# Cross attention and a feed-forward layer on one core: the query projection as two levels of Strassen's product, in four PSUM streams

## The chip, the core and the metric

The kernel runs on one NeuronCore of a Trainium2 chip. Its engines work side by side, each through its own queue of instructions in order: TensorE (PE; its weight loads are listed as PEld), VectorE (DVE), ScalarE (ACT), GpSimd (POOL) and SyncE (SP), which here only starts transfers between DRAM and the on-chip memory SBUF. TensorE writes its products to PSUM, eight banks of 128 x 512 float32; VectorE and ScalarE take them out of there. Engines wait for each other by semaphores.

The metric is the device time of one execution in microseconds (us), as a median of several. A profile is one more execution, recorded instruction by instruction; its span is a little shorter than its time.

## The reference

Everything is float32. x is 8 x 128 x 512 (8 sequences of 128 tokens, 1024 tokens T), the context the same, with 32 heads of 128.

```python
def reference(x, ctx, mask, position_bias, ln_weight, w_q, w_k, w_v, w_out, Wg, Wu, Wd, ag, au, ad):
    h = layernorm(x)
    n = rmsnorm(h) * ln_weight
    q = (n @ w_q.T).reshape(b, 128, 32, 128)          # w_q, w_k, w_v: 4096 x 512
    k = (ctx @ w_k.T).reshape(b, 128, 32, 128)
    v = (ctx @ w_v.T).reshape(b, 128, 32, 128)
    score = einsum('bqhd,bkhd->bhqk', q, k) + position_bias
    p = masked_softmax(score, mask)
    attn = einsum('bhqk,bkhd->bqhd', p, v).reshape(b, 128, 4096)
    x = x + h + attn @ w_out.T
    y = layernorm(x)
    return x + ((silu(y @ Wg.T * ag) * (y @ Wu.T * au)) @ Wd.T) * ad
```

## The kernel before

Weights and context arrive with the contracted dimension first, so that a product needs no transposition but that of the normed tokens. The 32 heads go in 8 groups of 4; a group's weights for the queries, keys or values are one tile of 128 x 4 x 512 (1 MB).

All projections use one level of Strassen's product in Winograd's form (`seven`, L210): weights and tokens are cut into 2 x 2 blocks, sums of blocks are made first (`sums_a` L191 for weights, `sums_b` L199 for tokens), and seven block products, not eight, are added up in the output. For a group's queries (`project_T`, L254), a block of weights holds 256 contracted rows and 256 outputs, a block of tokens 256 contracted rows and 512 tokens; a block product is two output tiles by two contracted chunks, each a matmul 128 x 128 by 128 x 512, so a group has 28 matmuls. TensorE runs a float32 matmul as two passes: the profile lists 448 for the queries. One bank of PSUM takes products 1, 6, 7 and 4 in turn, each added to what is there, and is read out after each; another takes product 2, a third 5 and 3. Products 2, 6, 7, 4 are copied out by ScalarE (L235, L245), products 1, 5 and 3 added by VectorE (L240, L251). Tiles come in pairs, so TensorE fills one bank while the other is read.

The stages, in order:

1. Keys and values of group 0. In between, layer norm and RMS norm of the tokens (`norm1`, L159), their transposition on TensorE (`norm1_T`, L178) into `hT` (128 x 7 x 1024: four chunks of normed tokens and three of sums).
2. Queries of all groups, L412 to L422. Weights come from a pool of three tiles (`wpool`), two groups ahead where a tile is free; GpSimd makes a group's four weight sums (`combine_rows`, L206); the finished heads go to DRAM, four transfers of 512 KB a group, since SBUF can't hold them. In the last round the keys' weights of group 1 are loaded (`load_kv`).
3. Attention, group by group (`probabilities` L290, `transpose_p` L331, `attend` L350), with the keys and values of the next group between. A score needs queries (from DRAM), keys and bias: GpSimd adds bias and mask (L296), VectorE adds the scores (L304), then softmax, a transposition of the probabilities through DRAM, and the product with the values.
4. Output projection, residual, second norm, feed-forward.

`acts` is a pool of 18 tiles of 128 x 1024 for whatever is large and short-lived: inputs, heads, keys, values. `work` holds temporaries of the norm and of attention. PSUM has three pools of two tiles (`ps_mm`, `ps_tp`, `ps` with two tags). Instructions are put into each engine's queue by a scheduler, which takes them in about the order of the program but may move them; a tile is given out again when all that read it have finished, and the engine that writes it next waits for that. SyncE's transfers are issued in the order of its queue: one that waits holds up all behind it.

The weight sums on GpSimd (`eng` is GpSimd):

```python
    def sums_a(eng, a11, a12, a21, a22, s1, s2, s4):
        eng.tensor_tensor(s1, a21, a22, ADD)
        eng.tensor_tensor(s2, s1, a11, SUB)
        eng.tensor_tensor(a21, a11, a21, SUB)
        eng.tensor_tensor(s4, a12, s2, SUB)
        return {1: a11, 2: a12, 3: s4, 4: a22, 5: s1, 6: s2, 7: a21}
```

Of the kernel before, what the change touches and what calls it, by code (L numbers as in the profile page):

```python
# [25 lines left out]
def xattn_ffn_kernel(  # L26
# [45 lines left out]
    acts = pool("acts", 18, reuse_waits="tile")  # L72
    work = pool("work", 2, side="right", reuse_waits="tile")
    small = pool("small", 4, side="right", reuse_waits="tile")

    proj, rows, attn = ExitStack(), ExitStack(), ExitStack()
    toks = pools(proj)("toks", reuse_waits="tile")
    spool = pools(proj)("spool", 2, reuse_waits="tile")
    wpool = pools(proj)("wpool", 3, reuse_waits="tile")
    hpool = pools(rows)("hpool", side="right", reuse_waits="tile")  # L80
    ps_mm, ps_tp, ps = (pools(attn)(f"ps{n}", 2, space=PSUM) for n in ("mm", "tp", "at"))

# [9 lines left out]
    def load_q(g):  # L92
        return load_w(f"wq{g}", wqT[:, bass.ts(g, GW)])

    ctx_sb = toks.tile([P, DC + 3, T], F32, tag="ctx", name="ctx_sb")
    wk0 = wpool.tile([P, DC, GW], F32, tag="w", name="wk0")
    wv0 = wpool.tile([P, DC, GW], F32, tag="w", name="wv0")

# [20 lines left out]
    for b in range(B):  # L121
        nc.sync.dma_start(x_in[b // 2][:, b % 2, :], x[b])
    q_w = {0: load_q(0)}

    lnw_sb = const.tile([P, DC], F32, name="lnw_sb")
    nc.gpsimd.dma_start(lnw_sb, lnw.rearrange("(c p) -> p c", p=P))
    mask_u8 = work.tile([P, B, S], U8, tag="tt", name="mask_u8")
    nc.gpsimd.dma_start(mask_u8, mask.rearrange("b q k -> q b k"))
# [25 lines left out]

    hT = hpool.tile([P, DC + 3, T], F32, tag="hT", name="hT")
    mv1 = const.tile([P, B, 2], F32, name="mv1")
    rs1 = const.tile([P, B], F32, name="rs1")

    def norm1(b):  # L159
        st = small.tile([P, nc.vector.BN_STATS_DIM], F32, tag="st", name=f"st_{b}")  # L160
        xb = x_in[b // 2][:, b % 2, :]
        moments(mv1, b, st, xb)
        rs = rs1[:, b : b + 1]
        rstd_of(rs, mv1[:, b, 1:2], 1.0)
        y = work.tile([P, D], F32, tag="s", name=f"y_{b}", bufs=3)
        nc.vector.tensor_scalar(
            y, xb, mv1[:, b, 0:1], rs, ALU.subtract, ALU.mult
        )
        sq = work.tile([P, D], F32, tag="aT", name=f"sq_{b}")
        ss = small.tile([P, 1], F32, tag="ss", name=f"ss_{b}")  # L170
        nc.scalar.activation(sq, y, AF.Square, accum_out=ss)
        rr = small.tile([P, 1], F32, tag="rr", name=f"rr_{b}")
        rstd_of(rr, ss, 1.0 / D)
        hn = work.tile([P, D], F32, tag="pT", name=f"hn_{b}", bufs=4)
        nc.scalar.activation(hn, y, AF.Copy, scale=rr)
        return b, hn

    def norm1_T(b, hn):  # L178
        tp = transposed(hn, ps_tp.tile([P, DC, P], F32, tag="pt", name="tp"))
        nc.vector.tensor_tensor(  # L180
            hT[:, :DC, bass.ts(b, S)], tp, lnw_sb.unsqueeze(2).to_broadcast([P, DC, P]), ALU.mult
        )

# [22 lines left out]

    def combine_rows(name, w):

        a11, a12 = w[:, :HC, :HW], w[:, HC:, :HW]
        a21, a22 = w[:, :HC, HW:], w[:, HC:, HW:]  # L210
        s = spool.tile([P, 3, HC, HW], F32, tag="S", name=f"S_{name}")
        s1, s2, s4 = s[:, 0], s[:, 1], s[:, 2]
        return sums_a(nc.gpsimd, a11, a12, a21, a22, s1, s2, s4)

# [38 lines left out]

    def project_T(name, w, src, heads):  # L254

# [12 lines left out]

        yield from seven(name, range(2), product, part, ps_mm)

    def project_V(name, w, src, pairs, *banks):
# [16 lines left out]

        yield from seven(name, range(2), product, part, *banks)


# [79 lines left out]
    def kv(g, out):  # L371
        wk, wv = kv_w.pop(g)
        kT, v = [], []
        out[g] = kT, v
        keys = project_T(f"k{g}", combine_rows(f"k{g}", wk), ctx_t, kT)
        if g:
            yield from keys
            yield from project_V(f"v{g}", combine_rows(f"v{g}", wv), ctx_t, v, ps_mm)
        else:

            yield from itertools.islice(keys, 4)
            values = project_V(f"v{g}", combine_rows(f"v{g}", wv), ctx_t, v, ps, "sc")
            yield from itertools.islice(values, 4)
            yield from keys
            yield from values
# [6 lines left out]
    for n, _ in enumerate(kv(0, kvs)):  # L392
        if n % 2 == 1 and 5 <= n < 5 + 2 * B:
            normed.append(norm1((n - 5) // 2))
        if n % 2 == 1 and 11 <= n < 11 + 2 * B:
            norm1_T(*normed.pop(0))
    for n in normed:
        norm1_T(*n)
    h_t = combine_tokens(hT)

# [6 lines left out]
    for t, src in ((ag_sb, ag), (au_sb, au)):  # L407
        nc.sync.dma_start(t[:, :nf], src[: nf * P].rearrange("(c p) -> p c", p=P))
        if INTER % P:
            nc.sync.dma_start(t[: INTER % P, nf : nf + 1], src[nf * P :].unsqueeze(1))  # L410
    nc.sync.dma_start(ad_sb, ad.partition_broadcast(P))
    for g in range(NG):  # L412
        if g + 1 < NG:
            q_w[g + 1] = load_q(g + 1)
        else:
            kv_w[1] = load_kv(1)
        heads = []
        for _ in project_T(f"q{g}", combine_rows(f"q{g}", q_w.pop(g)), h_t, heads):
            pass
        for j in range(GH):  # L420
            nc.sync.dma_start(queries[g][:, j, :], heads[j])

    rows.close()

# [337 lines left out]
```

## Time and profile before

| | |
|---|---|
| time, median of 3 runs | 1153.86 us (1151.64 to 1154.1) |
| profiled execution | 1155.07 us |
| its span | 1153.3 us |
| TensorE busy | 1116.4 us, 97% |
| VectorE, ScalarE, GpSimd busy | 501.0, 317.4, 307.3 us |
| chain that ended last | 90% TensorE; 17% of the span is `mm_q` L261 |
| query stage | 69.2 to 261.5 us, one group 24 us |

The page counts busy time by engine and follows back the chain of waits that ended last. Groups of instructions give a line of the program, engine, operation, output and inputs with shapes, how often, busy time and the mean of one, and the idle time in front of them with what ended it. TensorE's ends are modelled, so spacing is a better measure of a matmul than its listed length: matmuls are pipelined, and a listed 592 ns of a 512-column pass overlaps its neighbours.

### The profile page before, as it was taken

Reading aid. Unit: us, or ns where it says so; the run is one execution under the profiler, and the core shown is the slowest. Engines: PE = TensorE matmul, PEld = TensorE weight load, DVE = VectorE, ACT = ScalarE, POOL = GpSimd, SP = SyncE. Lnnn points to the kernel's source line nnn. Section 1 sums busy time; section 2 is a strip of 40 time slices with the busy share of each in tenths; the row PEclk is TensorE's granted clock in tenths of the full one; section 3 lists DMA queues with packets and bytes.
Section 4 is the critical chain, followed back from the end, with each engine's and each line's share of the span. In section 5 each row is a group of like instructions: output and inputs, shape, how many; then the busy total and the mean of one; then the engine's idle time right before and its main releaser. Section 6 shows DMA issues by size and latency. Waiting matters only on the chain.

```text
span 1153.3 us, 12296 instructions
## 1 busy us (share of the span) xinstructions
PE 1116.4 (97%) x4286; PEld 729.4 (63%) x4286; DVE 501.0 (43%) x937; ACT 317.4 (28%) x889; POOL 307.3 (27%) x255
## 2 busy tenths in 40 slices
PE   6899999999999999999999999689999999999998
PEld 3564444445867677686858688578888864444445
DVE  4541111116555556555555557724433253433311
ACT  2521112223444344434344433301000022222000
POOL 5331221116333333333223314530000034330000
PEclk9999999999999999999999999899999999999999
DMA  9114423257646465555554446864222322110000
GB/s 281 43 37 149 178 110 110 109 204 252 187 138 200 145 192 162 176 181 174 184 172 148 135 146 199 256 217 170 92 92 80 116 99 73 36 37 1 15 31 28
DMA packets 117534, 154.38 MB, mean 134 GB/s; under 512 B 12033, under 2 KB 71681, under 8 KB 117473
## 3 DMA queue, kind: packets, MB, share of 16 engines
q1 hardware_dynamic: 114784, 149.93, 40.4%
q10 hardware_dynamic: 2192, 2.10, 0.6%
q0 software_dynamic: 496, 1.58, 0.4%
q8 instruction: 34, 0.56, 0.2%
q14 instruction: 28, 0.22, 0.1%
HBM read 101.14 MB, written 52.43 MB: 133 GB/s over the span
## 4 chain that ended last, share of the span: by engine, by line
PE 90%; DVE 4%; DMA 4%; issue 1%; ACT 1%; SPq 0%; ACTq 0%; DVEq 0%
PE mm_q L261 17%; PE mm_v L279 16%; PE mm_k L261 15%; PE m L469 15%; PE mm_f L688 9%; PE dn L712 7%; PE sc L301 4%; PE av L357 4%; DMA turned<-tt 1%; DMA wk<-in_wkT_dram 1%; DVE sg L640 1%; DMA a<-att 1%; DVE act L643 1%; PE tp L152 1%; PE up L654 1%
## 5 line engine op out<-in xcount | busy, mean ns | idle before, releaser
L296 POOL TENSOR_TENSOR s<-pb,mneg 128x512 f32<-128x512 f32 x64 | 81.2, 1269 | 290.7 <-DVE tt L334 234.0
L261 PE MATMUL mm_k<-ctx_sb,wk 128*128 128x512 f32 x256 | 117.4, 603 | 7.5 <-DMA wk<-in_wkT_dram 4.4
L279 PE MATMUL mm_v<-wv,ctx_sb 128*128 128x256 f32 x512 | 115.9, 379 | 1.3 <-DMA wv<-in_wvT_dram 1.3
L261 PE MATMUL mm_q<-hT,wq 128*128 128x512 f32 x256 | 112.5, 592 | 0.0
L469 PE MATMUL m<-wo,a 128*128 128x256 f32 x400 | 100.6, 389 | 9.6 <-DMA a<-att 9.1
L311 ACT ACTIVATE s<-s,nmx 128x128 f32<-128x128 f32 x256 | 99.5, 390 | 37.4 <-DVE nmx L308 37.4
L279 PEld LDWEIGHTS mm_v<-wv,ctx_sb 128*128 128x128 f32 x512 | 95.1, 190 | 14.8 <-DMA wv<-in_wvT_dram 2.1
L362 ACT COPY aT<-av 128x512 f32<-128x512 f32 x64 | 37.5, 586 | 202.9 <-PE av L357 98.5
L261 PE MATMUL mm_k<-ctx_sb,S_k 128*128 128x512 f32 x192 | 87.8, 605 | 4.4 <-DVE k L240 4.0
L469 PEld LDWEIGHTS m<-wo,a 128*128 128x128 f32 x400 | 77.1, 196 | 21.2 <-DMA a<-att 9.5
L261 PEld LDWEIGHTS mm_q<-hT,wq 128*128 128x128 f32 x256 | 48.6, 190 | 60.8 <-issue 60.7
L279 PE MATMUL mm_v<-S_v,ctx_sb 128*128 128x256 f32 x384 | 86.4, 381 | 0.0
L261 PEld LDWEIGHTS mm_k<-ctx_sb,wk 128*128 128x128 f32 x256 | 46.9, 193 | 60.4 <-issue 45.2
L261 PE MATMUL mm_q<-hT,S_q 128*128 128x512 f32 x192 | 85.0, 592 | 0.0
L304 DVE TENSOR_TENSOR s<-sc,s 128x512 f32<-128x512 f32 x64 | 44.2, 690 | 86.0 <-PE sc L301 82.9
L301 PEld LDWEIGHTS sc<-k,q 128*128 128x128 f32 x512 | 67.4, 194 | 17.9 <-issue 13.4
L279 PEld LDWEIGHTS mm_v<-S_v,ctx_sb 128*128 128x128 f32 x384 | 71.7, 190 | 10.6 <-DVE v L251 1.5
L712 PE MATMUL dn<-wd,act 128*128 128x512 f32 (+3 forms) x198 | 75.8, 545 | 0.0
L251 DVE TENSOR_TENSOR q<-q,mm_q 128x512 f32<-128x512 f32 x32 | 22.0, 688 | 114.8 <-PE mm_q L261 114.8
L301 PE MATMUL sc<-k,q 128*128 128x128 f32 x512 | 68.1, 277 | 2.8 <-DMA q<-queries 2.8
L357 PE MATMUL av<-pT,v 128*128 128x128 f32 x512 | 67.9, 277 | 0.0
L261 PEld LDWEIGHTS mm_k<-ctx_sb,S_k 128*128 128x128 f32 x192 | 35.6, 193 | 48.6 <-issue 35.7
(156 smaller groups left out, 1494.3 us busy)
## 6 DMA issues: line engine op xcount, KB each, us to landing
queries<-q SPq DMA_DIRECT2D x32, 512.0 KB, 3.8
q<-queries SPq DMA_DIRECT2D x32, 512.0 KB, 4.5
turned<-tt SPq DMA_DIRECT2D x64, 256.0 KB, 2.2
pT<-turned SPq DMA_DIRECT2D x256, 64.0 KB, 2.5
att<-aT SPq DMA_DIRECT2D x64, 256.0 KB, 2.3
a<-att SPq DMA_DIRECT2D x32, 512.0 KB, 3.4
wq<-in_wqT_dram SPq DMA_DIRECT2D x8, 1024.0 KB, 5.6
wk<-in_wkT_dram SPq DMA_DIRECT2D x7, 1024.0 KB, 6.2
```

The costliest lines, as they stand in the source:

```text
L251: nc.vector.tensor_tensor(part(r, c, t), part(r, c, t), m[t], ADD)
L261: nc.tensor.matmul(out, w[i][:, c, bass.ts(t, P)], src[i][:, c, :], start=(first and c == 0), stop=(c == HC - 1), skip_group_check=True,)
L279: nc.tensor.matmul(out[:, bass.ts(k, HW)], src[i][:, c, bass.ts(2 * t + k, S)], w[i][:, c, :], start=(first and k == 0 and c == 0), stop=( ...
L296: nc.gpsimd.tensor_tensor(s, pb, mneg[:, b : b + 1, :].to_broadcast([P, GH, S]), ALU.add)
L301: nc.tensor.matmul(sc[:, j, :], qT[:, j, bass.ts(b % 2, S)], kT[j][:, cols], start=True, stop=True)
L304: nc.vector.tensor_tensor(s, sc, s, ALU.add)
L311: nc.scalar.activation(s[:, j, :], s[:, j, :], AF.Exp, bias=nmx[:, j : j + 1], accum_out=sm[:, j : j + 1],)
L357: nc.tensor.matmul(av[:, j, :], v[b // 2][:, b % 2, bass.ts(j, P)], pT[:, :, j, :], start=True, stop=True,)
L362: nc.scalar.copy(aT, av)
L469: nc.tensor.matmul(m[n], sa[n][:, c, :], wo_t[g][n][:, c, :], start=(g == order[0] and c == 0 and k % 2 == 0), stop=(g == order[-1] and c ...
L688: nc.tensor.matmul(out, ws[t][n][:, c, :], h2_t[n][:, c, :], start=(first and c == 0), stop=(c == HC - 1), skip_group_check=True,)
L712: nc.tensor.matmul(o, act[ic][:m, bass.ts(b, S)], wd[:m, ic, cols], start=(n == 0), stop=(n == NI - 1),)
```

## The change

The query projection gets a second level: each of the seven block products is again cut into 2 x 2 and done as seven products, so a group has 49 products, each one matmul of 128 x 128 by 128 x 256 (one contracted chunk, one output tile, a quarter of the tokens). Each level saves one product in eight, so 49 replace 56 half-width ones.

The work around it changes with it:

- `hT` becomes 128 x 7 x 7 x 256: 7 outer by 7 inner blocks of tokens. `combine_tokens2` makes the outer sums and the inner ones, eight more VectorE instructions and one more on GpSimd, besides four (three of them on VectorE) that are made while the norm still runs.
- `combine_rows2` makes twelve weight sums a group on GpSimd in place of four: the outer four, four inner ones of the raw blocks, four of the three outer sums. It is called one group ahead. Weights, and all sums of them, are in two pools `qw`, group g in pool g % 2.
- `project_T2` runs the inner products as the outer loop (k = 2, 1, 6, 7, 4, 5, 3) and, for each, the seven outer products in four streams: A holds products 2 and 1, B 6 and 7, C 4 and 5, D product 3, each with two banks of PSUM. After each k the four banks are read out, ScalarE and VectorE as before. What is kept is not heads but seven outer products in eight `acts` tiles (`kept`).
- The outer additions (12 on VectorE, 2 on GpSimd per group) and eight stores of 256 KB per group form a list, which the next group's call works off.
- The stage's pools lie where those of attention come later, so `wpool`, `spool`, `work` and attention's PSUM pools are opened after it. The keys and values weights of group 1 and the bias are thus loaded after the stage; the keys of group 0 go to DRAM and come back; the mask is loaded into an `acts` tile.

```diff
-    q_w = {0: load_q(0)}
-    mask_u8 = work.tile([P, B, S], U8, tag="tt", name="mask_u8")
+    mask_u8 = acts.tile([P, B, S], U8, tag="a", name="mask_u8")
     nc.gpsimd.dma_start(mask_u8, mask.rearrange("b q k -> q b k"))
...
-    hT = hpool.tile([P, DC + 3, T], F32, tag="hT", name="hT")
+    hT = hpool.tile([P, 7, 7, 256], F32, tag="hT", name="hT")
...
+    def inner_tokens(v):
+        nc.vector.tensor_tensor(v[:, :, 4], v[:, :, 1], v[:, :, 0], SUB)
+        nc.vector.tensor_tensor(v[:, :, 5], v[:, :, 3], v[:, :, 4], SUB)
+        nc.vector.tensor_tensor(v[:, :, 6], v[:, :, 2], v[:, :, 5], SUB)
+    def inner_last(eng, v):
+        eng.tensor_tensor(v[:, :, 1], v[:, :, 3], v[:, :, 1], SUB)
+    def combine_tokens2():
...
+        nc.vector.tensor_tensor(quad(4), quad(1), quad(0), SUB)
+        nc.vector.tensor_tensor(quad(5), quad(3), quad(4), SUB)
+        nc.gpsimd.tensor_tensor(quad(1), quad(3), quad(1), SUB)
+        nc.vector.tensor_tensor(quad(6), quad(2), quad(5), SUB)
+        inner_last(nc.gpsimd, hT[:, 0:3:2])
+        for v in (hT[:, 4:7], hT[:, 1:4:2]):
+            inner_tokens(v)
+            inner_last(nc.vector, v)
+    def combine_rows2(name, w, pool):
+        outer = combine_rows(name, w, pool)
...
+        four = inner(lambda k, r: raw[:, :, :, k, r], *(i4[:, n] for n in range(3)))
+        rest = inner(lambda k, r: three[:, :, k, bass.ts(r, P)], *(i3[:, n] for n in range(3)))
...
+    STREAMS = {"A": (2, 1), "B": (6, 7), "C": (4, 5), "D": (3,)}
+    INNER = ((2, 1, 1), (1, 1, 1), (6, 1, 2), (7, 2, 2), (4, 2, 1), (5, 2, 2), (3, 1, 2))
+    def project_T2(name, w, dst, before):
+        for n, (k, r, c) in enumerate(INNER):
+            for tag, pair in STREAMS.items():
...
+                m = banks[tag]
+                for h, i in enumerate(pair):
+                    nc.tensor.matmul(
+                        m[:, h], w(i, k), hT[:, BLOCK[i], BLOCK[k]],
+                        start=(k in (2, 1, 5) and h == 0), stop=True, skip_group_check=True,
+                    )
...
+                to = kept[tag, r][:, c - 1]
+                if k in (1, 5, 3):
+                    nc.vector.tensor_tensor(to, to, m, ADD)
+                else:
+                    nc.scalar.copy(to, m)
+            if k not in (1, 5, 3):
+                for _ in range(6):
+                    if before:
+                        before.pop(0)()
...
+        for r in (1, 2):
...
+            add(nc.vector, m[2], m[1])
+            store(m[2], 0, 0, r)
+            add(nc.vector, m[6], m[1])
+        for r in (1, 2):
...
+            add(nc.vector, m[7], m[6])
+            add(nc.vector, m[6], m[5])
+            add(nc.gpsimd, m[5], m[7])
+            store(m[5], 1, 1, r)
+            add(nc.vector, m[4], m[7])
+            store(m[4], 1, 0, r)
+            add(nc.vector, m[6], m[3])
+            store(m[6], 0, 1, r)
+        return todo
...
+    keys0 = dram.tile([P, GH, T], F32, name="keys0")
+    for j in range(GH):
+        nc.sync.dma_start(keys0[:, j], kvs[0][0][j])
...
+    left, rows = [], combine_rows2("q0", load_q(0), qw[0])
     for g in range(NG):
+        now = rows
         if g + 1 < NG:
-            q_w[g + 1] = load_q(g + 1)
-        else:
-            kv_w[1] = load_kv(1)
-        heads = []
-        for _ in project_T(f"q{g}", combine_rows(f"q{g}", q_w.pop(g)), h_t, heads):
-            pass
-        for j in range(GH):
-            nc.sync.dma_start(queries[g][:, j, :], heads[j])
-    rows.close()
+            rows = combine_rows2(f"q{g + 1}", load_q(g + 1), qw[(g + 1) % 2])
+        left = project_T2(f"q{g}", now, queries[g], left)
+    for do in left:
+        do()
+    first.close()
...
+    kv_w[1] = load_kv(1)
+    for j in range(GH):
+        kvs[0][0][j] = acts.tile([P, T], F32, tag="a", name=f"k0_{j}")
+        nc.sync.dma_start(kvs[0][0][j], keys0[:, j])
```

## The prediction, made before the changed kernel ran

> **What bounds the kernel now.** I read the chain of waits first, in order of time, because it says which engine ended each stretch.
>
> ```profile
> 65.76 3.46 PE mm_v L279 x16
> 69.22 192.27 PE mm_q L261 x448
> 261.48 0.89 PE sc L301 x8
> ```
>
> Columns: start, length, what. TensorE alone makes up the query stage, from 69.2 to 261.5 us: 192.27 / 448 = 429 ns for one pass over 512 columns. The values' passes over 256 columns, each with fresh weights, take 3.46 / 16 = 216 ns, so half-width passes stream at the same rate; the weight load (190 ns in the groups of instructions) fits under them. The table by stage shows the other engines nearly idle in one 24 us group (117 to 141): VectorE 4.12 us, ScalarE 4.69, GpSimd 4.98. Next, what the helpers cost:
>
> ```profile
> L195 POOL TENSOR_TENSOR wq<-wq 128x512 f32<-128x512 f32 x8 | 10.1, 1268 | 0.0
> L195 POOL TENSOR_TENSOR wg<-wg 128x256 f32<-128x256 f32 x5 | 3.6, 730 | 0.0
> L717 DVE TENSOR_TENSOR r<-r,x 128x512 f32<-128x512 f32 x7 | 4.8, 691 | 0.2
> L245 ACT COPY q<-mm_q 128x512 f32<-128x512 f32 x48 | 28.1, 586 | 81.7 <-PE mm_q L261 81.7
> ```
>
> Busy time, then the mean of one in ns. And from the transfers, size and median us from issue to landing:
>
> ```profile
> wq<-in_wqT_dram SPq DMA_DIRECT2D x8, 1024.0 KB, 5.6
> ...
> wv<-in_wvT_dram SPq DMA_DIRECT2D x7, 1024.0 KB, 7.0
> ```
>
>  A GpSimd sum of 512 columns costs 1.27 us (starts 1.22 apart back to back), of 256 0.73, so 384 is about 1.0 (0.95 apart). VectorE sums start 0.60 apart. In the timelines of VectorE and GpSimd at the stage's start, both read two SBUF operands:
>
> ```profile
> 68.49 2.99 DVE L202 TENSOR_TENSOR hT<-hT 128x1024 f32<-128x1024 f32 x1
> ```
>
> ```profile
> 68.06 2.35 POOL L203 TENSOR_TENSOR hT<-hT 128x1024 f32<-128x1024 f32 x1 [11.93 <-DVE hT L201]
> 70.37 2.25 POOL L193 TENSOR_TENSOR S_q<-wq 128x512 f32<-128x512 f32 x1
> ```
>
> The VectorE sum, 1.23 us alone, waits for the GpSimd one to end at 70.4; the next GpSimd sum, 1.27 alone, then takes 2.25. They take turns. Last, the table by stage around TensorE's longest wait, 3.96 us up to 26.08 for VectorE's first keys addition (the last three columns: granted clock, DMA share, GB/s):
>
> ```profile
> 25.00:30.00 5.00, 3.92 (x6) 1.74 (x7) 5.00 (x17) 1.96 (x7) 5.00 (x5) 0.66 0.70 157
> ```
>
> A clock of 0.66 over 5 us: a wait this long costs another 0.34 x 5 = 1.7 us of matmul time.
>
> **What the change takes away.** 8 x 49 products, two passes each, are 784 passes x 216 ns = 169.6 us against 192.3: **-22.7 us**, 21.2 us a group. Only TensorE gains.
>
> **The new weight chain.** Per group GpSimd now does 4 outer sums of 512, 4 inner of 512, 4 inner of 384, then two additions for the results of the previous group. In the order in which the built program's instructions stand, SyncE's queue holds: load of weights g+2, eight stores of group g, load of g+3. Two of the stores wait for the two GpSimd additions; GpSimd does these only after all twelve sums for g+2, which wait for the load of g+2. So load, twelve sums, two additions, stores and next load form a ring, one turn per group. A turn P is:
> - five stores issued after the additions, 0.4 each (issues of this size take 0.32 to 0.38 and stand some 0.06 apart): 2.1 with the semaphore;
> - the load: 5.6 alone; it stands behind 1.25 MB of stores. The first weight load, behind eight input loads, took 7.4, value loads up to 10.1. I take 6.8, as its backlog is partly drained when it is issued;
> - sums 8 x 1.22 + 4 x 0.95 + 0.15 = 13.7;
> - VectorE's twelve SBUF sums per group: about five fall into GpSimd's stretch, 0.6 each: 3.0. Bounds 0 and 5.0 (eight);
> - two additions 2.5 and hops 0.2.
>
> Sum **P = 28.3 us**, bounds 24.1 and 33.7, against 21.2 of matmuls. Even the lower bound is above, so the ring sets the pace from group 3 on and TensorE waits.
>
> What TensorE waits for: the pool of 18 activation buffers, 4 held by the values, 8 filled per group. Group g's B copies on ScalarE (second stream, first round) need the buffer of group g-2's C results, freed only by those late stores. Behind that copy stand ScalarE's C and D copies, VectorE's B addition and stream B's product 6 on TensorE. From the additions' end to the end of that group's matmuls: 3.2 (stores issued and landed; 256 KB stores land in 2.2 to 2.3) + 1.4 (copy 0.59, addition 0.69, hops) + 33 products x 0.43 = 14.3 + 1.7 for the clock after the idle = 20.6.
>
> The Trainium skill (SBUF — State Buffer, "Who interferes with whom") has a VectorE instruction with two SBUF inputs and a GpSimd one that reads SBUF exclude each other for the whole instruction. Charged for all twelve sums at the trace's 0.69, that would be 8.3 us a turn instead of 3.0, so P 33.6 and a time near 1223 instead of 1197.
>
> **The start.** The mask's load was GpSimd's second instruction, at 2.17 us, landed by 9.55. It now stands behind six sums for keys and values and the context sum, about 26.7 us; with 3.6 to 7.4 to land (the software-queue loads), VectorE's mask instruction, now ahead of the first keys addition, ends at 31 to 35. That addition ran at 25.26; TensorE and ScalarE's norm chain hang on it. The idle of 3.96 us grows by 5.6 to 9.3; I take **+7**. Afterwards TensorE had no slack up to 69.2.
>
> Then the token sums: VectorE did 3 sums of 1024 after the last transposed tile; it now does those plus four of 512 and four of 768 (0.6, 0.88 apart: 5.9 us) before the first round's additions, which round three needs. From the trace the third sum of 1024 ends near 73.2; the rest at 79.1 alone, 85 if each waits for a GpSimd sum. Two rounds of TensorE from 69.2 end at 75.3: stall 4.6 to 10.5, **+8**, nearer the upper as GpSimd starts its sums at 75.
>
> **Adding up the stage**, in the old time scale (the +7 comes on top): group 0 ends at 69.2 + 21.2 + 8 = 98.4. Load 5.6, twelve sums 13.7, contention 1.5, one addition 1.2: additions of group 0 end at 120.4. Group 1's: two stores 0.8, load 5.9, sums 16.7, additions 2.5: 146.4. Four turns of 28.3: 259.6. Last matmuls: +20.6 = 280.2 against 261.3: **+18.9**.
>
> **The end of the stage.** Value weights 1 and bias used to be loaded during the stage. Both now wait for the stage's buffers, and on SyncE's queue for the last stores, thus for VectorE's ten last sums: 0.7 + 6.0 + 1.2 for turns with GpSimd = 7.9 after the last matmul; value load issued at 8.4, landed (7.4) at 15.8. GpSimd takes two value sums before the first bias + mask: 2.6 + 1.25; VectorE's scores 0.7; the third score product can go at 20.5. Until then TensorE has 1.8 of scores and 3.4 of keys: idle 15.3, where it idled 0.45 before; and 1.7 for the clock. **+17**, bounds 8 (the bias, landing in 3.3, not held up by the value loads and sums, and no loss of clock) and 20 (value load 10.1).
>
> Costed at nothing: the keys' round trip through DRAM (eight transfers of 512 KB, 3.8 and 4.5 us), issued twenty and more us ahead; ScalarE's copies (8.5 us a group) and VectorE's 6.5 + 7.2 us, under 28 us; hT written in halves (8 x 0.15 us), under the values' matmuls. Had that cover gone, the last is 1.2 us.
>
> **Sum**: 7 + 18.9 + 17 = +42.9 on the profiled execution's 1155.07 (span 1153.3 and 1.8 around it): 1198. That execution stands 1.2 above the median of 1153.86; I say **1197**.
>
> **Rivals.**
> - *The matmuls keep the pace, the ends cost what I say*: -22.7 + 8 + 7 + 17 = +9.3, 1164. For it: transfers overlap well elsewhere (131 GB/s here, 363 and more at the start). Against: GpSimd's fourteen instructions and one load alone are 13.7 + 2.5 + 5.6 = 21.8 > 21.2.
> - *Faster*: the ring stays hidden, in one place: if the loads land early enough that P is at most 21.2, the whole 22.7 comes home, and the ends at their lower bounds (4.6 + 5.6 + 8 = 18.2) leave -4.5: 1150.6. It decides only from P = 21.2 down and with ends under 22.7 in sum.
> - *The turn-taking is heavier, or loads crawl behind the stores*: P = 33.7, each turn +5.4, about five turns: +27, 1224. For it: the 2.25 and 2.99 us rows; against: most VectorE sums come when GpSimd awaits its load.
>
> **Chances and range.** Mine (1175 to 1214) 0.62; heavier turns 0.14; matmul pace with dear ends (1156 to 1175) 0.16; faster 0.06; no change 0.02. A difference counts from 0.2% (2.3 us), about what this kernel's measurement can tell. All lower bounds together give 1161, all upper ones 1237; both ends at once are unlikely: **1163 to 1224**.
>
> **What would show it.** In the new profile: mm_q passes of 216 ns, with TensorE idle in each group from the third on, put down to VectorE or ScalarE behind a store; weight loads one per 28 us; GpSimd sums near 1.27 with some at 1.9; the mask sum on VectorE after 30 us; TensorE idle some 15 us in the 20 us after the last mm_q. Group starts 21 us apart would make the forecast wrong, and so would weight loads issued while the twelve sums run.

## The result, and the profile after

The changed kernel takes 1208.36 us (median of four runs, 1202.59 to 1208.73) where the kernel before, run beside it, takes 1153.98: a ratio of 1.046, with a 95% interval of 1.0429 to 1.0491. It is slower by 54.4 us in the medians. The profiled execution is the fastest of the four, 1202.59 us (span 1200.8), which is 47.5 us above the profiled one of before; the working below goes by that one.

From the page of the kernel after, the busy times and the chain that ended last:

```profile
PE 1116.1 (93%) x4622; PEld 803.4 (67%) x4622; DVE 626.5 (52%) x1100; ACT 343.8 (29%) x953; POOL 422.9 (35%) x336
...
PE 69%; DVE 6%; DMA 3%; issue 1%; POOL 1%; ACT 1%; SPq 1%; DVEq 0%; ACTq 0%; POOLq 0%
```

TensorE was 97% busy and is 93%. The 69% of the chain can't be set beside the 90% of before: here the chain is followed back to 217.3 us only, and its shares add up to 82%. TensorE is busy as long as before (1116.1 us, before 1116.4), though it has less to do. In the stage it is busy 183.2 us where it was 192.4, and 13.9 us of that are more than the products need; in the hand-over to attention it is busy 37.1 where it was 30.4. The mean granted clock is 0.94 and 0.80 there, where both were 1.00: after the wait of 8.02 us below it is 0.50 and 0.58 for two microseconds each. Where it waits, from its timeline (start, length, what, and in brackets the idle time in front and what ended it):

```profile
32.27 5.64 PE L263 MATMUL mm_k<-ctx_sb,S_k 128*128 128x512 f32 x8 [11.33 <-DVE rs L143]
94.09 2.08 PE L357 MATMUL mm_q_A<-hT,i_q 128*128 128x256 f32 x4 [8.02 <-DVE q_A L367]
185.62 1.27 PE L357 MATMUL mm_q_A<-hT,i_q 128*128 128x256 f32 x4 [3.79 <-DVE q_A L367]
188.92 2.08 PE L357 MATMUL mm_q_B<-hT,i_q 128*128 128x256 f32 x4 [2.03 <-DVE q_B L367]
312.88 1.65 PE L416 MATMUL sc<-k,q 128*128 128x128 f32 x6 [9.80 <-DVE s L419]
```

Three places: the keys at the start (idle 3.96 us before, 11.33 now), the queries (group 0, little in groups 1 to 3, then every group from 4 on), and the first scores after the stage. Their shares follow from three moments of the two traces: the first query product starts at 69.05 before and 74.69 after (+5.6); from there to the end of the last one it is 192.4 us before and 214.2 after (+21.8, though 784 half passes of 216 ns are only 169.3); from there to the first values product of group 1 it is 30.9 before and 51.8 after (+20.9). That is 48.3, of which 0.8 comes back by the end.

One turn of the stage, on SyncE's queue and on GpSimd, in the timeline of the kernel after:

```profile
187.06 0.46 SPq L93 DMA_DIRECT2D wq<-in_wqT_dram  x1
193.66 1.28 POOL L195 TENSOR_TENSOR S_q<-wq 128x512 f32<-128x512 f32 x1 [9.93 <-DMA wq<-in_wqT_dram]
207.39 0.99 POOL L198 TENSOR_TENSOR i_q<-S_q,i_q 128x384 f32<-128x384 f32 x1
208.34 3.39 POOL L377 TENSOR_TENSOR q_C<-q_C,q_B 128x512 f32<-128x512 f32 x2
210.08 2.55 SPq L380 DMA_DIRECT2D queries<-q_C  x3
214.56 0.68 SPq L93 DMA_DIRECT2D wq<-in_wqT_dram  x1
```

The reader is to see the ring close: a load at 187.06, its first sum 6.6 us later, twelve sums to 208.34, two additions, the stores, and the next load at 214.56, 27.5 us after the first. It is the shortest of the three turns from the load at 157.75 to that at 243.87, which take 28.7 us in the mean. Their loads take 6.6 to 7.1 us to the first sum, the sums 14.7 to 16.0, additions and stores 6.2 to 6.7. The groups of instructions, from 75 to 290 us, show that TensorE waits for something else as well (busy time, mean ns, then the idle time in front and its releasers):

```profile
L357 PE MATMUL mm_q_B<-hT,i_q 128*128 128x256 f32 x96 | 28.6, 426 | 4.3 <-DVE q_B L367 4.3
L357 PE MATMUL mm_q_A<-hT,i_q 128*128 128x256 f32 x96 | 28.2, 420 | 24.1 <-DVE q_A L367 24.1
...
L369 ACT COPY q_B<-mm_q_B 128x512 f32<-128x512 f32 x32 | 18.8, 586 | 52.4 <-DMA queries<-q_C 38.2 <-PE mm_q_B L357 13.5 <-DVE q_C L367 0.7
```

ScalarE's B copy stands behind the late stores (38.2 us). TensorE's own idle time is 24.1 us for VectorE's addition of stream A, 8.0 of it in group 0, against 4.3 for that of stream B. These figures do not say which wait costs more, for the one on A comes first and hides most of the one on B. In group 4, whose two waits are shown above, ScalarE's timeline has:

```profile
187.56 0.59 ACT L369 COPY q_B<-mm_q_B 128x512 f32<-128x512 f32 x1 [10.29 <-DMA queries<-q_C]
```

The B copy starts when a store has landed, and B's product can't go before 188.92, had A been ready or not. Groups 5 and 6 are alike (copies at 214.78 and 244.10, products at 216.14 and 245.46); in group 7 the wait on A ends last, by half a microsecond. Read so, the ring does set the pace of this kernel, as forecast, and a second wait, for VectorE, lies just in front of it. The experiments had to find out what VectorE was doing there.

### The profile page after: what moved, and what is told of

Its sections match the earlier page's. It is cut to its first block, busy times and chain, and to the rows that moved or that the text cites. A ratio compares the mean times of both kernels' runs of the same rounds, so it can differ in the third digit from the quotient of the medians.

```text
span 1200.8 us, 13514 instructions
## 1 busy us (share of the span) xinstructions
PE 1116.1 (93%) x4622; PEld 803.4 (67%) x4622; DVE 626.5 (52%) x1100; ACT 343.8 (29%) x953; POOL 422.9 (35%) x336
## 3 DMA queue, kind: packets, MB, share of 16 engines
q1 hardware_dynamic: 128736, 154.12, 40.4%
## 4 chain that ended last, share of the span: by engine, by line
PE 69%; DVE 6%; DMA 3%; issue 1%; POOL 1%; ACT 1%; SPq 1%; DVEq 0%; ACTq 0%; POOLq 0%
PE m L601 15%; PE mm_v L281 14%; PE mm_k L263 13%; PE mm_f L820 8%; PE dn L844 6%; PE av L472 4%; PE sc L416 4%; DMA x<-in_x_dram 1%; DVE q_B L377 1%; DVE sg L772 1%; PE mm_q_C L357 1%; PE mm_q_B L357 1%; PE mm_q_A L357 1%; DVE act L775 1%; DMA wv<-in_wvT_dram 1%
## 5 line engine op out<-in xcount | busy, mean ns | idle before, releaser
L263 PE MATMUL mm_k<-ctx_sb,wk 128*128 128x512 f32 x256 | 121.6, 619 | 7.5 <-DMA wk<-in_wkT_dram 6.6
L416 PE MATMUL sc<-k,q 128*128 128x128 f32 x512 | 70.2, 282 | 15.4 <-DVE s L419 12.8
L263 PEld LDWEIGHTS mm_k<-ctx_sb,S_k 128*128 128x128 f32 x192 | 35.8, 194 | 55.5 <-issue 47.5
L844 PEld LDWEIGHTS dn<-wd,act 128*128 128x128 f32 (+1 forms) x198 | 37.6, 190 | 38.5 <-issue 37.4
L472 PEld LDWEIGHTS av<-pT,v 128*128 128x128 f32 x512 | 62.6, 192 | 0.7 <-issue 0.5
L601 PE MATMUL m<-T_o,S_a 128*128 128x256 f32 x224 | 58.5, 384 | 1.4 <-DVE S_a L196 1.4
L357 PE MATMUL mm_q_A<-hT,i_q 128*128 128x256 f32 x96 | 28.2, 420 | 24.1 <-DVE q_A L367 24.1
```

The costliest lines, as they stand in the source:

```text
L263: nc.tensor.matmul(out, w[i][:, c, bass.ts(t, P)], src[i][:, c, :], start=(first and c == 0), stop=(c == HC - 1), skip_group_check=True,)
L357: nc.tensor.matmul(m[:, h], w(i, k), hT[:, BLOCK[i], BLOCK[k]], start=(k in (2, 1, 5) and h == 0), stop=True, skip_group_check=True,)
L416: nc.tensor.matmul(sc[:, j, :], qT[:, j, bass.ts(b % 2, S)], kT[j][:, cols], start=True, stop=True)
L472: nc.tensor.matmul(av[:, j, :], v[b // 2][:, b % 2, bass.ts(j, P)], pT[:, :, j, :], start=True, stop=True,)
L601: nc.tensor.matmul(m[n], sa[n][:, c, :], wo_t[g][n][:, c, :], start=(g == order[0] and c == 0 and k % 2 == 0), stop=(g == order[-1] and c ...
L844: nc.tensor.matmul(o, act[ic][:m, bass.ts(b, S)], wd[:m, ic, cols], start=(n == 0), stop=(n == NI - 1),)
```

## The experiments

Each ran beside the kernel before, and its ratio is to that. "Turn" is the mean distance of the last four weight loads (three intervals) in its one profile; it is 28.7 us after the change, and 29.2 to 29.7 in the three versions below that leave the ring as it is (`mask_early`, `start_sums`, `handover`).

**The ring's links.** Two single cuts, and both together. In `additions_vector` VectorE makes the two additions that SyncE's stores wait for:

```diff
-            add(nc.gpsimd, m[5], m[7])
+            add(nc.vector, m[5], m[7])
```

> The two GpSimd additions of each group are made by VectorE; all else stays. Theory R (the ring: weight load, twelve GpSimd sums, GpSimd's two additions, stores on SyncE's queue, next weight load): the stores no longer stand behind the sums, so a load waits only for its buffer, that is for the end of the matmuls two groups back. Load 6.5 + twelve sums 14.7 = 21.2, with hops 21.5 to 23.5 us from load to load in place of 28.7; about five turns make -26 to -36 us, and the hand-over loses the 5.3 us of two contended additions: 1168 to 1182 against 1208. Rival V (VectorE's turns with GpSimd set the pace): VectorE now has fourteen sums of SBUF operands in place of twelve, so loads stay 27 us apart or more, and the time at 1200 or above. Rival B (the 18 activation buffers, whoever does the addition): 25 to 27 us, 1185 to 1200.

1203.06 us, ratio 1.0413 [1.0398, 1.0429]; turn 27.6. In `loads_scalar` the loads leave SyncE's queue:

```diff
-        nc.sync.dma_start(w, wqT[:, bass.ts(g, GW)].rearrange("(c p) n -> p c n", p=P))
+        eng = nc.scalar if g > 1 else nc.sync
+        eng.dma_start(w, wqT[:, bass.ts(g, GW)].rearrange("(c p) n -> p c n", p=P))
```

> The weight loads of groups 2 to 7 are issued by ScalarE's queue, so they no longer stand behind the stores on SyncE's; the additions stay on GpSimd. Theory R: the link from stores to load is gone, but the C results are still stored only after the twelve sums of two groups on, and their buffers gate the B copies: two turns take 6.8 (load) + 14.7 (sums) + 3.4 (additions) + 3.2 (stores) + 20.6 (to the end of the matmuls) = 48.7, so 24.3 a turn, -4.4 a turn, about -18 to -24 us: 1184 to 1190 against 1208. If the queue order is all, and the buffers don't bind, the matmuls' 21.2 us set the pace: -35 to -40, 1170. If the queue is no link at all (rival B or V): within 5 us of 1208.

1209.38 us, 1.0471 [1.0449, 1.0493]; turn 28.1.

> Both edits together: additions on VectorE, loads of groups 2 to 7 on ScalarE's queue. Theory R: no link is left, and the loads come as the matmuls free their buffers: 21.2 to 22.5 us from load to load, 1164 to 1176, what the additions alone give or up to 6 us less. Rival V: VectorE's turn-taking holds it above 25 us a turn, 1190 or more.

1206.26 us, 1.0445 [1.0427, 1.0462]; turn 27.6. The ring was cut, and next to nothing came home: what I had expected of theory R fell short by some 20 to 40 us in all three, and rival V (27 us a turn or more, 1200 or above) is what came. TensorE's waits on B are gone in all three profiles, and those on A are 4.3 to 4.8 us in groups 2 to 6. The timeline of `both_links` shows why (VectorE, GpSimd and TensorE in one group):

```profile
164.78 3.42 DVE L378 TENSOR_TENSOR q_B<-q_B 128x512 f32<-128x512 f32 x2
165.95 1.71 POOL L196 TENSOR_TENSOR i_q<-wq 128x512 f32<-128x512 f32 x1
168.13 3.14 DVE L378 TENSOR_TENSOR q_B<-q_B,q_C 128x512 f32<-128x512 f32 x2
169.02 1.71 POOL L197 TENSOR_TENSOR i_q<-i_q,wq 128x512 f32<-128x512 f32 x1
171.20 0.68 DVE L368 TENSOR_TENSOR q_A<-q_A,mm_q_A 128x512 f32<-128x512 f32 x1
172.02 1.89 PE L358 MATMUL mm_q_A<-hT,i_q 128*128 128x256 f32 x4 [4.77 <-DVE q_A L368]
```

VectorE's sums of two SBUF operands take 1.7 us each, and GpSimd's 1.71 instead of 1.27, while the addition of a PSUM operand (L368) takes 0.68 in the middle of it. Six such sums, which the scheduler has put at the head of the group, hold up the second round's addition until 171.2, and TensorE's third round waits 4.77 us for it. Then four passes take 1.89 us instead of 1.03, at a granted clock of 0.55 and then 0.60 for two microseconds each, which loses 1.7 us. 21.2 of matmuls + a mean wait of 4.6 + 1.7 are 27.5 of the turn's 27.6. So there were two chains of nearly one length, 28.7 through the ring and 27.6 through VectorE's queue, and cutting the first uncovers the second.

Group 7 of the same trace is the counter-test. GpSimd has no weights left to sum (it is idle from 259.9 to 299.95), and VectorE has the same six sums at the head of the group, from 271.93 to 275.54:

```profile
273.13 1.28 DVE L378 TENSOR_TENSOR q_B<-q_B 128x512 f32<-128x512 f32 x2
274.33 1.28 DVE L378 TENSOR_TENSOR q_B<-q_B,q_C 128x512 f32<-128x512 f32 x2
```

They take 3.6 us where they took 9.4, and TensorE does not wait for VectorE in this group. Order, stores and buffers are those of the groups before, and only the weight load is missing besides, on which this addition does not hang. So it is the turns with GpSimd that make this wait.

**Shorter GpSimd sums.** Four of the twelve weight sums left out:

```diff
-        rest = inner(lambda k, r: three[:, :, k, bass.ts(r, P)], *(i3[:, n] for n in range(3)))
...
-                return rest[k][:, {5: 0, 6: 1, 3: 2}[i]]
+                return three[:, {5: 0, 6: 1, 3: 2}[i], k % 2, bass.ts(k // 4, P)]
```

> The four inner weight sums of 384 columns of each group are left out (the products of the outer sums take raw blocks of them instead, so those values are not the reference's). Theory R: GpSimd's sums are a link of the ring, so each turn falls by just what they took, 4 x 0.95 to 1.1 us: 28.7 to 24.5 or so, about five turns and the first load: -20 to -25 us, 1183 to 1188. If GpSimd's sums are no link (rivals B and V), the turn stays within 1 us, apart from what VectorE waits less for them: 1202 or above.

The four runs lie between 1187.09 and 1211.89 us, too far apart to give this version a time. Three lie where the rivals had put it, the fourth where theory R had (1183 to 1188); it has no profile, and why it is 20 us below the others stays open. The profile is of an execution of 1209.59 us; in it the turn is 28.4, and TensorE waits 4.96 or 4.97 us for VectorE's stream A addition in four groups running (170.62, 199.86, 228.14, 255.94). A third of GpSimd's sums gone, and the same wait at the same place: in this execution it is again VectorE's chain, not the ring.

**VectorE's order.** On top of both cuts, VectorE's outer additions are queued behind its additions of round two (seven) and round six (seven); `last` is the addition just made:

```diff
+        def outer(n):
+            with tc.issue_after(last.ins):
+                for _ in range(n):
+                    if before:
+                        before.pop(0)()
...
+            if k == 1:
+                outer(9)
+            if k == 5:
+                outer(99)
-            if k not in (1, 5, 3):
-                for _ in range(6):
-                    if before:
-                        before.pop(0)()
```

> As both_links, and VectorE's outer additions of the group before are queued behind its additions of the second round (seven of them) and of the sixth (seven), in place of six at the group's start. Theory V (with both links of the ring gone, TensorE waits 4.4 to 4.8 us a group for VectorE's second-round addition, which stands behind six sums of SBUF operands that take 1.7 us each in turns with GpSimd, and loses some 1.7 us more to the clock): the wait goes, the turn falls from 27.6 to 21.5 to 23 us, five turns and a half: -25 to -34 us against both_links, 1172 to 1181. Rival: the turn is held by loads, stores or buffers that share the DMA queues, not by VectorE's order: 1200 or above.

1202.11 us, 1.0416 [1.0364, 1.0468]; turn 27.4: the expectation failed. In the profile the 4.6 us wait is down to 0.6, but another has come, 2.1 us for ScalarE's D copy, which needs a buffer that the second batch of seven frees, and most of those still take 1.7 us each because GpSimd's next sums have just begun. The rest of the 27.4 is the clock, at 0.68, 0.50, 0.50 and 0.61 for two microseconds each from 194 on, 3.4 us lost.

**The sums themselves.** The fourteen outer additions left out, everything else kept, loads on ScalarE's queue:

```diff
-            todo.append(lambda: eng.tensor_tensor(a, a, b, ADD))
+            return
```

> The fourteen outer additions of each group are left out (the stores send the products as they are), loads of groups 2 to 7 on ScalarE's queue: GpSimd still makes all twelve weight sums, and every transfer stays. Theory V: VectorE has no sums of SBUF operands left, GpSimd's sums stand 1.22 us apart, the turn is the matmuls' 21.2 to 22 us, and the hand-over loses the eight us of additions after the last matmul: 1160 to 1170. Rival (transfers or GpSimd's own sums hold the turn): 25 us or more a turn, 1190 or above.

1169.04 us, 1.0124 [1.0095, 1.0154]. Its timeline, GpSimd and ScalarE's queue:

```profile
170.07 1.27 POOL L196 TENSOR_TENSOR S_q<-wq 128x512 f32<-128x512 f32 x1 [7.35 <-PE mm_q_B L358]
...
143.39 0.38 ACTq L94 DMA_DIRECT2D wq<-in_wqT_dram  x1
164.54 0.38 ACTq L94 DMA_DIRECT2D wq<-in_wqT_dram  x1
185.70 0.38 ACTq L94 DMA_DIRECT2D wq<-in_wqT_dram  x1
206.85 0.38 ACTq L94 DMA_DIRECT2D wq<-in_wqT_dram  x1
```

GpSimd's sums are back at 1.27 us, and loads come 21.15 us apart, the pace of 98 half passes of 216 ns. With all transfers and all weight sums still there, the stage is TensorE's again from group 1 on. Of the 37 us between this and `both_links`, 36 lie in the stage (181.5 us from first to last product, there 217.6). That is the price of VectorE's fourteen additions in this place, with all that hangs on them: the stores no longer wait for a sum, so the buffers come free earlier too, and this run alone does not part the one from the other.

**Buffers.** `sums_later`, and the values of group 0 go to DRAM during the stage, so that the queries have 18 buffers for the 16 of two groups:

```diff
+    values0 = dram.tile([P, B // 2, 2 * GW], F32, name="values0")
+    for i in range(B // 2):
+        nc.sync.dma_start(values0[:, i], kvs[0][1][i].rearrange("p a n -> p (a n)"))
...
+    for i in range(B // 2):
+        kvs[0][1][i] = acts.tile([P, 2, GW], F32, tag="a", name=f"v0r_{i}")
+        nc.sync.dma_start(kvs[0][1][i].rearrange("p a n -> p (a n)"), values0[:, i])
```

> As sums_later, and the values of group 0 go to DRAM and come back after the stage, as the keys do, so that all 18 activation buffers serve the queries (two groups need 16). Theory: what is left in sums_later, 2.1 us a group for ScalarE's copy of stream D into a buffer that VectorE's last sums free, 0.6 for VectorE, and 3 or so of matmuls at half clock after that wait, is the buffers' doing: the turn falls from 27.5 to 21.5 to 24, 1170 to 1186 with the hand-over as dear as before. Rival: VectorE's fourteen sums in turns with GpSimd's twelve hold the turn, whatever the buffers: 26 us or more, 1196 to 1206.

1198.06 us, 1.0405 [1.0377, 1.0433]: the time stays in the rival's range, but the turn falls from 27.4 to 24.7. The stage, first product to last, takes 201.8 us instead of 215.6; the hand-over, with four more loads in it, gives most of it back (58 us from the last query product to the first values product, where it was 51.8). So the buffers were a third link, and 3.5 us a turn are left without it, most of it TensorE's waits of 2.4 to 3.6 us for VectorE's stream A addition.

**The start.** The mask's load on ScalarE's queue, ahead of the loads of x:

```diff
-    nc.gpsimd.dma_start(mask_u8, mask.rearrange("b q k -> q b k"))
+    nc.scalar.dma_start(mask_u8, mask.rearrange("b q k -> q b k"))
```

> The mask's load is issued by ScalarE's queue, before the loads of x, in place of GpSimd's after its first sums. If the mask shifts the whole start: VectorE's mask instruction no longer holds up its first keys addition, TensorE's wait of 11.3 us there falls to about 4, the query stage starts 5.5 us earlier and all behind it: 1201 to 1204 against 1208. Rival: the token sums on VectorE end when they did, as the norm sets them, and the gain is lost in TensorE's third round: within 2 us.

1204.37 us, 1.0432 [1.04, 1.0464], not told apart from the change's 1.046. VectorE's mask instruction runs at 18.46 instead of 29.89; TensorE's wait for the keys falls from 11.33 to 7.27 and the stage starts at 72.48 instead of 74.69. But the last weight load of the stage comes at 244.06, where it came at 243.87: the 2.2 us are used up on the way. The token sums, in `start_sums`: group 0's weight sums are made first, and four of the eight late token sums are queued behind VectorE's second round:

```diff
-        for v in (hT[:, 4:7], hT[:, 1:4:2]):
-            inner_tokens(v)
-            inner_last(nc.vector, v)
+        for v in vs:
+            nc.vector.tensor_tensor(v[:, :, 4], v[:, :, 1], v[:, :, 0], SUB)
+            nc.vector.tensor_tensor(v[:, :, 5], v[:, :, 3], v[:, :, 4], SUB)
+        def rest():
+            for v in vs:
+                inner_last(nc.vector, v)
+            for v in vs:
+                nc.vector.tensor_tensor(v[:, :, 6], v[:, :, 2], v[:, :, 5], SUB)
```

> At the start: the weight sums of group 0 are made before the token sums, so that they don't take turns, and the four token sums that only rounds four and five need are queued behind VectorE's additions of the second round. If the stall of 8.0 us ahead of TensorE's third round is VectorE's eight token sums in turns with GpSimd: it falls to 0 to 3, and as every later turn starts from group 0's end, the whole kernel gains 6 to 10 us: 1198 to 1202 against 1208. Rival: the ring's phase comes from GpSimd and the loads alone: within 2 us.

1206.06 us, 1.0449 [1.0423, 1.0475]: no gain. TensorE's timeline in that kernel:

```profile
87.10 2.07 PE L366 MATMUL mm_q_A<-hT,i_q 128*128 128x256 f32 x4 [4.10 <-DVE q_A L376]
115.88 1.37 PE L366 MATMUL mm_q_A<-hT,i_q 128*128 128x256 f32 x4 [4.62 <-DVE q_A L376]
```

The stall at group 0 is halved, 8.02 to 4.10, and group 1 then waits 4.62 where it waited 1.23. An early start is worth nothing ahead of a stage whose pace something else sets.

**The hand-over.** Weights of group 1 and the bias by ScalarE's queue ahead of the last additions, and three bias sums on VectorE:

```diff
+        eng = nc.scalar if name in ("wk1", "wv1") else nc.sync
+        eng.dma_start(t, src.rearrange("(c p) n -> p c n", p=P))
...
+    nc.scalar.dma_start(pb0, pbias[:GH].rearrange("h q k -> q h k"))
...
-        nc.gpsimd.tensor_tensor(
+        (nc.vector if g == 0 and b < 3 else nc.gpsimd).tensor_tensor(
             s, pb, mneg[:, b : b + 1, :].to_broadcast([P, GH, S]), ALU.add
```

> The keys and values weights of group 1 and the bias are loaded by ScalarE's queue, ahead of the last group's additions and stores in the program, and the first three sums of bias and mask are made by VectorE instead of GpSimd; the query stage itself stays. Theory (the hand-over is late because these loads stand behind the last stores on SyncE's queue, and the bias sums behind GpSimd's value sums): TensorE's waits of 2.6, 1.7 and 9.8 us after the last query product shrink to some 6 in sum, and with less loss of clock the kernel gains 8 to 13 us: 1195 to 1200 against 1208. Rival: VectorE's last ten additions, GpSimd's two and the scores' queries coming back from DRAM are late next: within 4 us.

1197.25 us, 1.0389 [1.0357, 1.042], as expected. From the last query product to the first values product it is 40.4 us, where the change has 51.8 and the kernel before 30.9. The chain of waits of the kernel after had named the link (start, length, what):

```profile
301.53 6.69 DMA wv<-in_wvT_dram
308.29 1.26 POOL S_v L195
309.62 1.26 POOL S_v L196
310.89 1.23 POOL s L411
312.14 0.70 DVE s L419
312.88 1.65 PE sc L416 x6
```

The values' weights stood behind the last stores on SyncE's queue, and the bias sum behind two sums of those weights.

**All together**, with the mask first on GpSimd's queue, ahead of the loads of weights and context:

```diff
+    nc.gpsimd.dma_start(mask_u8, mask.rearrange("b q k -> q b k"))
     lo, hi = slice(0, HW), slice(HW, GW)
```

> All the edits together: both ring links, sums_later's order, values away, the mask loaded first on GpSimd's queue, group 0's sums before the token sums and four token sums later, and the hand-over's loads on ScalarE's queue. If the terms add up: 1208 - 5 (mask) - 6 (token sums) - 25 to -33 (turns) - 10 (hand-over) = 1154 to 1162, level with the kernel before or up to 1% behind it; the matmuls' 22.7 us can't come home while the start and the hand-over keep a dozen. If VectorE and GpSimd in turns hold the stage at 26 us a group: 1180 to 1190.

1182.71 us, 1.0267 [1.0237, 1.0296]; turn 24.2: the best version, still slower than the kernel before, and the less hopeful of the two cases expected. TensorE's timeline:

```profile
25.88 5.17 PE L265 MATMUL mm_k<-ctx_sb,S_k 128*128 128x512 f32 x8 [4.20 <-DVE k L244]
288.45 5.54 PE L434 MATMUL sc<-k,q 128*128 128x128 f32 x32 [12.39 <-DMA q<-queries]
```

With the mask early, the keys wait 4.20 us (3.96 before) and the stage starts at 70.36. It ends at 265.0, 3.5 us behind the kernel before. What is left, 24 us, lies in the hand-over: the scores' queries are loaded at 281.08, behind the last store (280.44), and four loads of values, on their way back, stand between those stores. A last version, `apart`, leaves the values in SBUF, brings queries and keys back by ScalarE's queue, and delays each weight load behind a store, to keep GpSimd's sums out of VectorE's second batch:

```diff
+            if k == 1:
+                done = outer(10)
+                if later:
+                    with tc.issue_after(done[-1].ins):
+                        more = later()
```

> All edits but the values' trip to DRAM, and three more. Each weight load from group 2 on is queued on SyncE behind the store of the group before's first C result, 2 to 4 us later than in sums_later, so that GpSimd's twelve sums begin only when VectorE's second seven are done. The first scores' queries and the keys come back by ScalarE's queue ahead of the last additions and of the values' weights. The next weights are loaded after the last store. If the turn is long because VectorE's second batch meets GpSimd's sums: loads stand 21.5 to 24 us apart, where all_edits had TensorE waiting 2.4 us in most groups; the stage starts at 70.4 as there, loses 5.7 at group 0 and ends at 247 to 260 (before: 261); with a hand-over that costs 8 to 14 us more than before's: 1149 to 1168, at best level with the kernel before. If the exclusion costs the same wherever the sums are put (14 VectorE sums of 0.6 and 14.6 us of GpSimd are 23 us a group), or the buffers take over again: 25 us a turn, 1170 to 1185.

1203.49 us, 1.0426 [1.0408, 1.0445]; turn 27.9: a miss. In its timeline the load goes at 195.14, since VectorE was done with its first batch early, and the order that it was to bring about does not come:

```profile
201.94 1.27 POOL L196 TENSOR_TENSOR S_q<-wq 128x512 f32<-128x512 f32 x1 [11.10 <-DMA wq<-in_wqT_dram]
203.41 1.70 DVE L399 TENSOR_TENSOR q_C<-q_C,q_B 128x512 f32<-128x512 f32 x1
213.13 1.74 DVE L399 TENSOR_TENSOR q_B<-q_B,q_D 128x512 f32<-128x512 f32 x1
214.96 0.37 ACT L388 COPY q_D<-mm_q_D 128x256 f32<-128x256 f32 x1 [5.37 <-DVE q_B L399]
215.39 1.22 PE L376 MATMUL mm_q_D<-hT,S_q 128*128 128x256 f32 x2 [3.42 <-ACT q_D L388]
```

GpSimd starts 1.5 us ahead of the second batch, most of the batch runs at 1.7 us a sum, and the D copy waits for its buffer as in `sums_later`. Whether a placing that really keeps the two apart reaches the matmuls' pace was not tried.

## Why the prediction was right, and where it was not

The forecast was slower, 1197 in a range of 1163 to 1224; it is 1208.36. Of the 11.4 us between, 4.6 are the terms of the sum; 5.8 is that the profiled execution of the changed kernel lies that much below its median, and 1.0 the step from the profiled execution of before to its median:

| step | predicted | in the profile after |
|---|---|---|
| mask, start of the stage | +7 (5.6 to 9.3) | +5.6 |
| group 0's stall for the token sums | 8 (4.6 to 10.5) | 9.7 (8.02 + 1.49 + 0.15) |
| turn from group 3 on | 28.3 (24.1 to 33.7) | 28.7 |
| stage, first to last product | 211.0 | 214.2 |
| hand-over | +17 (8 to 20) | +20.9 |
| sum | +42.9 | +47.5 |

*The products.* 216 ns a half pass and 21.2 us a group held: `no_outer_additions` runs at 21.15 a group.

*The mask.* Right in place and nearly in size. The wait grew by 7.4 us (5.6 to 9.3 forecast), and the stage starts only 5.6 later, because TensorE did have slack behind it: the kernel before waits another 3.12 us up to 34.34, for ScalarE, and that wait is gone. With that load first on its queue (`all_edits`) 4.3 of the 5.6 are back.

*The ring.* The turn is right to 0.4 us, partly by luck in its parts: the sums took 15.4 us in the mean of three turns where 16.7 were charged (13.7, and 3.0 for turns with VectorE), additions and stores 6.4 where 4.6 were, the load 6.9 where 6.8 was. The path that was named is there too, from the late stores over the B copy to stream B. What the forecast did not see is a second chain beside the ring: a wait on stream A in front of the one on B. Cutting both links of the ring took 1.1 us off the turn, not the 6 to 7 that a lone ring would have given, since that chain alone makes 27.6.

*Costed at nothing.* Here lies the step that was wrong: VectorE's 6.5 + 7.2 us a group were called hidden under 28 us, by durations taken where GpSimd was nearly idle (4.98 us in 24). In turns with GpSimd, six sums at the head of a group take 9.4 us in `both_links` instead of 3.6, and TensorE waits for the addition behind them. Had the ring not covered it, the forecast would have been 6.4 us a group too low (27.6 against 21.2). That it didn't show in the time is luck.

*Turn-taking as a rival.* It was priced at 33.7 a turn, charged to GpSimd. The mechanism is real: in `both_links` an instruction of VectorE with two SBUF inputs and one of GpSimd go in pairs, 1.7 us to a pair, near the 0.60 + 1.22 that they need one after the other, and VectorE's additions from PSUM run through at 0.68. The Trainium skill (SBUF — State Buffer, "Who interferes with whom") says that a VectorE instruction with two SBUF inputs contends with a GpSimd instruction that reads SBUF, and these rows agree. But the price was on the wrong engine: GpSimd's twelve sums took 14.7 to 16.0 us a turn instead of the 13.8 that they need alone (`no_outer_additions`), and it was VectorE's queue that became late.

*Matmul pace as a rival* needed the turn at 21.2. By the forecast only transfers and sums stood against it. `no_outer_additions` keeps every transfer and all twelve GpSimd sums and reaches that pace, so it takes VectorE's additions, with what waits for them, to miss it.

*The hand-over.* The mechanism was right (`handover` gives 11.4 us of the 20.9 back by moving just those loads and sums). Two terms were too small. The last additions end 9.0 us after the last product, not 7.9, as GpSimd's two took 5.3 us in turns with VectorE's ten. Then the values' load goes only at 12.6, not 8.4, because issuing the stores ahead of it takes 3.6 us where 0.5 was charged; the load itself took 6.7 instead of 7.4.

Not settled: what parts the run of 1187 us of `fewer_sums` from its others, and with how much of the stage the chains of ring, buffers and VectorE's order each end up in a kernel where all three are present; they were cut in sequence, not each alone in every order.

## What to carry to other kernels

When a change adds sums on two engines that exclude each other on SBUF, add their times before comparing with the engine they are to hide under. Here, by an estimate from the times alone, 14 x 0.6 on VectorE and 13.8 on GpSimd are 22.2 us a group against 21.2 of matmuls. By that no order could have hidden them all, and none that was tried did; the 22.7 us saved on TensorE were bought with more than that. When a ring explains a turn to within half a microsecond, still look at the releaser of the bound engine's own waits: a second chain of nearly the same length makes every single cut look useless. And where two waits follow each other, the first hides the second: the larger idle time is not yet the longer chain. What a long stage had loaded ahead for the next one has to be paid at its end if its memory is taken away, and 20.9 us for that is as much as the stage itself lost.

## What the runs showed of the hardware

A wait can cost more than its length, because the granted clock of TensorE is lower after some waits. The table by stretch of `values_away`, behind a wait of 3.46 us up to 190.00, one of 2.41 us up to 165.15, and another of 3.46 us up to 240.33 (the last three columns: granted clock, DMA share, GB/s):

```profile
190.00:192.00 2.00, 2.00 (x7) 1.65 (x8) 2.00 (x4) 0.59 (x1) 2.00 (x2) 0.71 0.00 0
192.00:194.00 2.00, 2.00 (x6) 1.57 (x5) 2.00 (x2) 0.59 (x1) 2.00 (x3) 0.50 0.11 41
194.00:196.00 2.00, 2.00 (x10) 1.76 (x9) 2.00 (x3) 1.01 (x3) 2.00 (x2) 0.94 0.27 94
...
165.00:167.00 2.00, 1.85 (x9) 1.68 (x10) 2.00 (x5) 0.59 (x1) 2.00 (x2) 1.00 0.00 0
...
240.00:242.00 2.00, 1.67 (x8) 1.52 (x9) 2.00 (x5) 0.53 (x1) 2.00 (x3) 1.00 0.00 0
```

After the first wait the clock is at 0.71, 0.50 and 0.94 for two microseconds each, 2 x (0.29 + 0.50 + 0.06) = 1.7 us lost; after the other two it stays at 1.00. So the length of a wait alone does not decide it: two of 3.46 us in one trace end differently, and in the kernel after the change one of 2.94 us, up to 272.04, is followed by 0.50 while one of 2.95, up to 214.83, leaves 1.00. What does decide is not shown here. A group that waits twice (2.46 and 1.06 us in `apart`, up to 185.68 and 187.44) ran at 0.50 to 0.73 from 185.7 to 194.0.
